# The last part of a fused convolution, attention and expert kernel: the way back to channels on VectorE, reciprocal roots on ScalarE, and a new order

## The chip, the cores and the metric

The kernel runs on one core of a Trainium2 chip. The metric is device time in microseconds for one execution of the whole program; lower is better. The core has five engines that run their own instruction streams in order and wait for each other through semaphores: TensorE (PE in the profile; its weight loads are PEld), VectorE (DVE), ScalarE (ACT), GpSimd (POOL) and SyncE (SP, which here only issues DMAs).

## The reference, cut to what matters

The input is 32 images of 128 channels by 64 x 64 pixels. Two layers follow each other.

```python
# layer 0: a convolution in a butterfly basis, after a group norm
x = x + _kop2d(_gn(x), weight, kd1, kd2, k11, k12, k21, k22)
# layer 1: tokens are pixels, 128 channels each
t = to_tokens(x)
t = t + attn(_ln_t(t), Wk, bk, Wv, bv)                 # one 128 x 128 softmax per image
t = t + experts(_ln_t(t), router_w, router_b, expert_w, expert_b)   # 8 experts, the best 2 per token
x = from_tokens(t, x)

def _ln_t(v, eps=1e-5):
    m = jnp.mean(v, axis=-1, keepdims=True)
    s = jnp.var(v, axis=-1, keepdims=True)
    return (v - m) / jnp.sqrt(s + eps)
```

All is fp32. `_ln_t` needs the reciprocal root of a variance for each token (pixel), twice per image.

## The kernel before, in words

The program has three parts. The first brings every image into the butterfly basis along both axes, the second mixes channels there, and the third, which the change is in, takes one image at a time through the inverse transform, the attention and the experts. Parts hand over through DRAM (`xf`, `pf`).

The third part has, for each image `b`, these steps; their names are the keys that the plan below uses.

- `r0` to `r7` load the mixed image, `x` loads the original one (the tile is called `y` there). `w0` to `w7` (PE, L877, tile `pu`) invert along one axis, and `wo` (ACT, L887) copies the result to `u`, in four copies for each `pu`. `h0` to `h3` (PE, L899, tile `py`) invert along the other axis; every `py` needs all of `u`. `ho` (DVE, L907) adds the result to the image. For the first two images smaller pieces do the same.
- `pt0` to `pt7` (PE, L1021) transpose the image to tokens, four tiles of 128 tokens at a time, `to` (ACT, L1026) copies them to `tk`, which holds 32 tiles of 128 tokens x 128 channels, and `sa` (DVE, L993) takes batch statistics. `va` (DVE, L1003 to L1008) makes variances of them, `pwa` (POOL, L1013) the power of -0.5, `na` (DVE, L1050, L1051) what the normalization needs.
- `xg` (ACT, L1061) normalizes, `pg` (PE, L1072) sums the 128 x 128 Gram matrix, and a short chain (`gs`, `pb`, `t1`, `pb2`, `sm`, `pr`, `sr`, `sn`, `pc`, `prx`) makes the softmax of the attention.
- `pp` (PE, L1145) applies it, three token tiles at a time, `at` (ACT, L1158, L1162) scales, `ad` (DVE, L1173, L993) adds to `tk` and takes statistics. `vb`, `pwb`, `nb` make the second reciprocal root as `va`, `pwa`, `na` made the first.
- `lg`, `l2`, `f1` to `f4`, `gt` (DVE, L1205 to L1248, with one exponential on ACT, `f5`) make the gates of the best two experts.
- `xn` (ACT, L1273) normalizes, `px` (PE, L1283) transposes, `xT` (ACT, L1289) copies. `pe` (PE, L1296) multiplies one token tile with four experts; there are 64 such halves per image. `m` (DVE, L1307) weighs each half by the gates into `tm`, and `s` (POOL, L1332 to L1335) sums over experts into `tk`, once for two token tiles.
- `st` (PE, L1342, tile `po`) transposes four finished token tiles back to channels, `so` (ACT, L1348) copies them out of PSUM, and a DMA on SP's queue stores 128 channels x 512 pixels.

PSUM is shared by three pools: `pe` (three banks), `cv` (one buffer of two banks, for `pu` and `py`) and `tl` (three banks, for `pt`, `px`, `pp`, `po` and the small ones).

Steps of neighbouring images run beside each other: while image `b` is at its convolution, `b - 1` is at its attention and `b - 2` at its experts. The order of instructions on each engine is written by a planner (class `Plan`). Each step has an engine, a cost in microseconds that the author gave it, a due time (`SLOT` times the image's number, an offset and the step's entry in the table `SHIFT`), the steps it comes after, and buffers that it takes and frees. The planner plays the steps through with those costs, lets each engine take the ready step with the earliest due time, and the program is then emitted in that order. On the chip only the order is left: an engine waits at its next instruction, whatever else is ready.

Of the kernel before, what the change touches and what calls it, by code (L numbers as in the profile page):

```python
# [12 lines left out]
ALU = mybir.AluOpType  # L13
# [77 lines left out]
def kernel(  # L91
# [674 lines left out]
    rp = ctx.enter_context(tc.tile_pool(name="rp", bufs=10))  # L766
    xp = ctx.enter_context(tc.tile_pool(name="xp", bufs=2))
# [31 lines left out]
    def prepare():  # L799
# [23 lines left out]
    plan = Plan({"cv": 1, "pe": 3, "tl": 3, "r": 10, "x": 2, "xg": NG, "xn": 2, "xT": 2, "tm": 2, "so": 2, "gate": 2})  # L823
# [3 lines left out]
        "ad": -0.15, "at": -0.25, "f": 0.71, "gs": -1.97, "gt": 0.71, "h": -0.24, "ho": -3.5, "kvp": 3.43,  # L827
        "kvq": -0.45, "l": 0.71, "lg": 3.61, "m": -0.32, "na": -1.87, "nb": -0.81, "pb": -1.97, "pc": -1.97,
        "pe": 0.16, "pg": -0.08, "pp": 0.19, "pr": -1.97, "prx": -1.97, "pt": -0.23, "pwa": -1.87, "pwb": 3.61,
        "px": 0.15, "r": -0.04, "s": 0.08, "sa": 1.29, "sm": -1.97, "sn": -1.97, "so": 2.13, "sr": -1.97,  # L830
        "st": 1.1, "t": -1.97, "to": 0.06, "va": -1.87, "vb": 3.61, "w": 0.28, "x": -0.68, "xT": -0.68,
        "xg": 0.21, "xn": 2.42,
# [12 lines left out]
    xs, rs, tile_of, first = {}, {}, {}, [prepare]  # L845
# [25 lines left out]
    def conv(b):  # L871
# [31 lines left out]

        def h_out(g):
            def run():
                acc = xs[b][:, :, 16 * g : 16 * g + 16]
                nc.vector.tensor_tensor(  # L907
                    acc, tile_of.pop(("cy", b, g)).rearrange("o (w h) -> o h w", h=n), acc, ALU.add
                )
            return run  # L910
# [33 lines left out]
        def h_out_piece(q):  # L944
            def run():
                acc = xs[b][:, :, 8 * q : 8 * q + 8]
                nc.vector.tensor_tensor(
                    acc, tile_of.pop(("cz", b, q)).rearrange("o (w h) -> o h w", h=n), acc, ALU.add
                )
            return run  # L950

        if b < 2:
# [10 lines left out]
            for g in range(4):  # L963
                for k in range(2):
                    at = b + 0.68 + 0.07 * g + 0.035 * k
                    h, ho = (f"h{g}", f"ho{g}") if k else (f"h{g}_0", f"ho{g}_0")
                    add(
                        b, h, "PE", 1.05, at, h_inverse_piece(2 * g + k),
                        [f"wo{e}_{oh}" for e in range(8) for oh in range(2)] + ([f"h{g}_0"] if k else []), ("pe",),
                    )  # L970
                    add(b, ho, "DVE", 0.7, at, h_out_piece(2 * g + k), [h, "x"] + ([f"ho{g}_0"] if k else []), (), ("pe",))
# [9 lines left out]
        for g in range(4):  # L981
            at = b + 0.68 + 0.07 * g
            add(b, f"h{g}", "PE", 2.05, at, h_inverse(g), [f"wo{e}_{oh}" for e in range(8) for oh in range(2)], ("cv",))
            add(b, f"ho{g}", "DVE", 1.2, at, h_out(g), [f"h{g}", "x"], (), ("cv",))

    def front(b):
# [24 lines left out]
        def power(which):  # L1011
            total, var, nmr, rstd = v[which]
            nc.gpsimd.tensor_tensor(rstd, var, mhalf, ALU.pow)  # L1013

        def turn(g):
            def run():
                ps = tile_of["pt", b, g] = tps.tile([P, 512], F32, tag="tl", name=f"pt{b}_{g}")
                x1 = xs[b].rearrange("c h w -> c (h w)")
# [21 lines left out]
        for g in range(8):  # L1040
            at = s1 + 0.016 * g
            add(b, f"pt{g}", "PE", 0.48, at, turn(g), [(b - 2, f"st{g}")] + [f"ho{k}" for k in range(4)], ("tl",))
# [3 lines left out]
        add(b, "pwa", "POOL", 5.5, s1 + 0.14, lambda: power(1), ["va"])  # L1046

        def nmr1():
            total, var, nmr, rstd = v[1]
            nc.vector.scalar_tensor_tensor(nmr, total, -0.5, rstd, ALU.mult, ALU.mult)  # L1050
            nc.vector.tensor_scalar_add(v["above"], nmr, 1.0)  # L1051

        add(b, "na", "DVE", 0.9, s1 + 0.14, nmr1, ["pwa"])
# [85 lines left out]
        def product(lo, m):  # L1139
            def run():  # L1140
                x1 = xs[b].rearrange("c h w -> c (h w)")
# [35 lines left out]
        for j, lo in enumerate(range(0, NT, 3)):  # L1177
            m = min(3, NT - lo)
            at = s1 + 0.45 + 0.016 * j
            add(b, f"pp{lo}", "PE", 0.26 * m, at, product(lo, m), ["prx", (b - 1, "lg")], ("tl",), ("x",) if lo == 30 else ())  # L1180
# [29 lines left out]
        def nmr2():  # L1210
            total, var, nmr, rstd = v[2]
# [41 lines left out]
        add(b, "pwb", "POOL", 5.5, at, lambda: power(2), ["vb"])  # L1253
        add(b, "lg", "DVE", 1.95, at, logits1, ["vb"])
        add(b, "nb", "DVE", 2.1, at + 0.1, nmr2, ["pwb", "lg"])
# [8 lines left out]
    def experts(b):  # L1264
# [73 lines left out]
        def back(g):  # L1338
            def run():
                ps = tile_of["po", b, g] = tps.tile([P, 512], F32, tag="tl", name=f"po{b}_{g}")  # L1340
                for k in range(4):
                    nc.tensor.transpose(ps[:, k * P : (k + 1) * P], t[:, 4 * g + k, :], ident)  # L1342
            return run

        def store(g):
            def run():
                so = wp.tile([P, 512], F32, tag="so", name=f"so{b}_{g}")
                nc.scalar.copy(so, tile_of.pop(("po", b, g)))  # L1348
                nc.sync.dma_start(ov[b][:, g * 512 : (g + 1) * 512], so)
# [3 lines left out]
        for g in range(8):  # L1353
# [25 lines left out]
            add(b, f"st{g}", "PE", 0.48, at + 0.25, back(g), [f"s{2 * g}", f"s{2 * g + 1}"], ("tl",))  # L1379
            add(b, f"so{g}", "ACT", 0.55, at + 0.25, store(g), [f"st{g}"], (), ("tl",))  # L1380
# [63 lines left out]
```

## Time and profile before

| what | value |
| --- | --- |
| median of 3 runs | 6059.13 us (6056.47 to 6059.99) |
| profiled execution, span | 6062.4 us |
| PE busy | 5891.6 us |
| DVE busy | 4221.2 us |
| POOL busy | 4191.0 us |
| ACT busy | 3756.5 us |

The span is the time from the first to the last instruction of one profiled execution. A busy time is the sum of the engine's own instructions; matmuls overlap, and their ends are modelled. In lists of groups the columns are: line, engine, operation, written tile `<-` read tiles, shape and count, then busy microseconds in sum and mean nanoseconds of one, then the engine's idle time just before them and who ended it. In lists by time the columns are start, duration, engine, line, operation, and in brackets the idle time before. A matmul in fp32 shows as two instructions, a transpose as one.

### The profile page before, as it was taken

The numbers are of one execution on the slowest core, as the hardware profiler recorded it, in microseconds if no ns is written. First come the engines' busy times: TensorE is split into PE (matmuls) and PEld (weight loads), VectorE is DVE, ScalarE is ACT, GpSimd is POOL, SyncE is SP. The second block draws the span as 40 slices with busy tenths as digits, with TensorE's granted clock in tenths as the row PEclk, the third lists the DMA queues.
The fourth block names the chain that finished last, engine by engine and source line by source line (L and its number), as shares of the span: only waits on it lengthen the run. The fifth ranks groups of instructions, "written<-read, shape, count | busy, mean of one in ns | idle before, by whom it ended". The sixth has DMA issues, their size and how long they took to land.

```text
span 6062.4 us, 219265 instructions
## 1 busy us (share of the span) xinstructions
PE 5891.6 (97%) x95372; PEld 4677.6 (77%) x95372; DVE 4221.2 (70%) x7696; ACT 3756.5 (62%) x7057; POOL 4191.0 (69%) x3765
## 2 busy tenths in 40 slices
PE   7999999999999999889999999999999999999998
PEld 7999999999999999776666666666666666666654
DVE  5565545555555555448878787787878878787878
ACT  7666664555555555366667667666766766676663
POOL 2110006666666666428898898989989898998988
PEclk9999999999999999999999999999999999999999
DMA  6767666666666666632313222231322223132100
GB/s 200 238 224 237 234 214 193 172 173 172 172 174 171 171 171 172 160 107 77 92 56 102 67 88 81 72 97 57 101 68 84 84 64 104 57 97 71 65 27 28
DMA packets 555044, 756.74 MB, mean 125 GB/s; under 512 B 58592, under 2 KB 319712, under 8 KB 549984
## 3 DMA queue, kind: packets, MB, share of 16 engines
q1 hardware_dynamic: 551856, 738.76, 41.0%
q8 instruction: 749, 12.27, 0.9%
q0 software_dynamic: 896, 2.62, 0.1%
q14 instruction: 215, 1.76, 0.1%
q10 hardware_dynamic: 1328, 1.32, 0.1%
HBM read 406.93 MB, written 335.54 MB: 122 GB/s over the span
## 4 chain that ended last, share of the span: by engine, by line
PE 88%; ACT 7%; issue 2%; DVE 1%; POOL 1%; DMA 1%; SPq 0%; ACTq 0%; POOLq 0%; DVEq 0%
PE pe L1296 28%; PE m L654 17%; PE g L632 9%; PE pf L418 7%; PE pu L877 6%; PE pp L1145 4%; PE py L899 4%; PE pg L1072 4%; PE pv L396 3%; PE px L1283 2%; ACT xn L1273 2%; ACT u L887 2%; PE pz L373 1%; PE pt L1021 1%; ACT z L383 1%
## 5 line engine op out<-in xcount | busy, mean ns | idle before, releaser
L1296 PE MATMUL pe<-ew_sb,xT 128*128 128x512 f32 x4096 | 1948.4, 597 | 18.6 <-DVE tm L1307 15.1
L1307 DVE TENSOR_TENSOR tm<-pe,oh 128x512 f32<-128x512 f32 x2028 | 1346.6, 684 | 478.9 <-PE pe L1296 456.6
L1332 POOL TENSOR_TENSOR tm<-tm 128x512 f32<-128x512 f32 x1014 | 1285.0, 1284 | 202.6 <-DVE tm L1307 199.3
L1296 PEld LDWEIGHTS pe<-ew_sb,xT 128*128 128x128 f32 x4096 | 701.6, 191 | 523.4 <-issue 400.1
L643 DVE COPY f<-g 128x1024 f32<-128x1024 f32 x508 | 622.3, 1225 | 644.4 <-PE g L632 644.2
L654 PE MATMUL m<-f,s 128*64 128x64 f32 x32768 | 1068.9, 224 | 1.1 <-ACT f L643 0.8
L654 PEld LDWEIGHTS m<-f,s 128*64 128x64 f32 x32768 | 999.0, 138 | 62.4 <-issue 1.5
L600 POOL COPY s<-l 128x512 f32<-128x512 f32 x512 | 547.2, 1105 | 526.4 <-issue 509.7
L643 ACT COPY f<-g 128x1024 f32<-128x1024 f32 x508 | 514.7, 1013 | 556.4 <-PE g L632 530.1
L1335 POOL TENSOR_TENSOR tk<-tk,tm 128x256 f32<-128x256 f32 x1014 | 753.9, 743 | 79.5
L1333 POOL TENSOR_TENSOR tm<-tm 128x512 f32<-128x512 f32 x507 | 650.3, 1283 | 39.8
L887 ACT COPY u<-pu 64x512 f32<-64x512 f32 x960 | 556.3, 579 | 135.1 <-PE pu L877 121.6
L632 PE MATMUL g<-c,wst 9*128 9x128 f32 x16256 | 599.6, 283 | 1.7 <-issue 1.5
L632 PEld LDWEIGHTS g<-c,wst 9*128 9x128 f32 x16256 | 503.0, 186 | 36.2 <-issue 1.5
L349 POOL TENSOR_TENSOR grstd<-gms,mhalf 128x1 f32<-128x1 f32 x32 | 17.8, 555 | 737.8 <-DVE gms L345 737.8
L1158 ACT ACTIVATE pp<-pp,m 128x128 f32<-128x128 f32 x1024 | 440.9, 431 | 124.2 <-PE pp L1145 99.2
L602 POOL TENSOR_SCALAR s<-l 128x512 f32<-128x512 f32 x256 | 511.3, 1997 | 0.0
L877 PEld LDWEIGHTS pu<-qw,r 128*128 128x128 f32 x3840 | 455.1, 193 | 62.8 <-ACT u L887 49.0
L877 PE MATMUL pu<-qw,r 128*128 128x128 f32 x3840 | 475.8, 277 | 25.1 <-ACT u L887 25.1
L1289 ACT COPY xT<-px 128x512 f32<-128x512 f32 x256 | 150.2, 587 | 563.2 <-PE px L1283 560.1
L418 PE MATMUL pf<-ph,v 128*128 128x128 f32 x4096 | 491.2, 278 | 6.2 <-issue 1.4
L418 PEld LDWEIGHTS pf<-ph,v 128*128 128x128 f32 x4096 | 467.0, 192 | 16.0 <-ACT z L383 7.1
(169 smaller groups left out, 8569.6 us busy)
## 6 DMA issues: line engine op xcount, KB each, us to landing
xf<-f SPq DMA_DIRECT2D x512, 256.0 KB, 3.3
pf<-o SPq DMA_DIRECT2D x1024, 128.0 KB, 3.3
l<-xf SPq DMA_DIRECT2D x1012, 128.0 KB, 3.2
r<-pf SPq DMA_DIRECT2D x504, 256.0 KB, 4.7
x<-in_x_dram SPq DMA_DIRECT2D x256, 256.0 KB, 4.5
y<-in_x_dram SPq DMA_DIRECT2D x32, 2048.0 KB, 9.3
out_dram<-so SPq DMA_DIRECT2D x256, 256.0 KB, 2.2
tw<-in_tw_dram SPq DMA_DIRECT2D x6, 384.0 KB, 7.5
```

Of the source, the lines that this page charges most:

```text
L418: nc.tensor.matmul(pl[:, j * P : (j + 1) * P], vs[b][:, 8 * g + j, :], ph.rearrange("h r m -> h (r m)"), start=True, stop=True,)
L600: nc.gpsimd.tensor_copy(dst, src)
L632: nc.tensor.matmul(pg[g // 2][:, g % 2, m * P : (m + 1) * P], wst[rows, 16 * half + 4 * t + m, :], c[rows].rearrange("r h k -> r (h k)"), ...
L643: copy(f.rearrange("i m (g o) -> i m g o", g=2), tile_of["g", w, half, t][k].rearrange("i g (o m) -> i m g o", o=4))
L654: nc.tensor.matmul(ps[hh * n : (hh + 1) * n, q, :], s[:, h].rearrange("i k b -> i (k b)")[:, B * r : B * r + n], f[:, h, r, :], start=(r = ...
L877: nc.tensor.matmul(ps[:, k, :], rs[b, e][:, k * P : (k + 1) * P], qw.rearrange("w r m -> w (r m)"), start=True, stop=True,)
L887: nc.scalar.copy(u[r * n : (r + 1) * n, :, oh * n + 8 * e : oh * n + 8 * e + 8], ps[oh * n : (oh + 1) * n, :, r * n : (r + 1) * n].rearran ...
L1296: nc.tensor.matmul(ps, tile_of["xT", b, i // 4][:, i % 4, :], ew_sb[:, es, :].rearrange("d e c -> d (e c)"), start=True, stop=True,)
L1307: nc.vector.tensor_tensor(tile_of["tm", b, i // 2][:, i % 2, es, :], tile_of.pop(("pe", b, i, half)).rearrange("p (e c) -> p e c", c=P), t ...
L1332: nc.gpsimd.tensor_tensor(tm[:, k, 0:4, :], tm[:, k, 0:4, :], tm[:, k, 4:8, :], ALU.add)
L1333: nc.gpsimd.tensor_tensor(tm[:, :, 0:2, :], tm[:, :, 0:2, :], tm[:, :, 2:4, :], ALU.add)
L1335: nc.gpsimd.tensor_tensor(t[:, lo : lo + 2, :], t[:, lo : lo + 2, :], tm[:, :, m, :], ALU.add)
```

## The change

It has three pieces. The way back to channels leaves PE and ACT: `so` becomes a block transpose on DVE, which swaps rows and columns inside blocks of 32 x 32, from `tk` straight to the tile that is stored, and a new step `os` on SP stores it with four DMAs. For this the pixels stand in another order within a token tile (4 rows of the image x 32 columns), so that `ho` no longer adds in place but writes a new tile, and the pools change: `r` 10 to 7 buffers, `x` 2 to 1, and a new pool `y` of 2. The power of -0.5 leaves POOL: ACT makes the exponential of -0.5 times the logarithm, and DVE refines it by one Newton step of three operations, ahead of `na` and `nb`. And the table `SHIFT` of due places is new.

```diff
-    rp = ctx.enter_context(tc.tile_pool(name="rp", bufs=10))
-    xp = ctx.enter_context(tc.tile_pool(name="xp", bufs=2))
+    rp = ctx.enter_context(tc.tile_pool(name="rp", bufs=7))
+    xp = ctx.enter_context(tc.tile_pool(name="xp", bufs=1))
+    yp = ctx.enter_context(tc.tile_pool(name="yp", bufs=2))
...
-    plan = Plan({"cv": 1, "pe": 3, "tl": 3, "r": 10, "x": 2, "xg": NG, "xn": 2, "xT": 2, "tm": 2, "so": 2, "gate": 2})
+    plan = Plan({"cv": 1, "pe": 3, "tl": 3, "r": 7, "x": 1, "y": 2, "xg": NG, "xn": 2, "xT": 2, "tm": 2, "so": 2, "gate": 2})
...
     SHIFT = {
-        "ad": -0.15, "at": -0.25, "f": 0.71, "gs": -1.97, "gt": 0.71, "h": -0.24, "ho": -3.5, "kvp": 3.43,
...
+        "ad": 1.200, "at": 4.424, "f": -1.562, "gs": 5.457, "gt": 1.265, "h": 3.849, "ho": 0.837, "l": 3.501,
+        "lg": 4.916, "m": -6.559, "na": -1.525, "nb": 2.094, "os": -8.513, "pb": -14.726, "pc": -5.745,
+        "pe": 0.195, "pg": -3.978, "pp": 0.047, "pr": 3.687, "prx": 0.077, "pt": 0.017, "pwa": -4.729,
+        "pwb": 2.491, "px": 0.184, "r": 2.416, "s": 18.080, "sa": 3.764, "sm": -3.600, "sn": -3.745,
+        "so": 2.421, "sr": 3.337, "t": -3.008, "to": -4.337, "va": -9.740, "vb": 0.270, "w": 2.015, "wo": 4.100,
+        "x": 9.338, "xT": 4.479, "xg": -7.285, "xn": 5.672,
     }
...
+        def added(ps, lo, m):
+            if lo == 0:
+                ys[b] = yp.tile([P, 16, 2, 4, 32], F32, tag="y", name=f"x1_{b}")
+            wh, j = divmod(lo, 32)
+            nc.vector.tensor_tensor(
+                ys[b][:, :, wh, :, j : j + m].rearrange("o l a w -> o a l w"),
+                ps.rearrange("o (w a l) -> o a l w", a=4, w=m),
+                xs[b][:, :, lo : lo + m].rearrange("o (a l) w -> o a l w", a=4), ALU.add,
+            )
...
         def power(which):
             total, var, nmr, rstd = v[which]
-            nc.gpsimd.tensor_tensor(rstd, var, mhalf, ALU.pow)
+            nc.scalar.activation(rstd, var, AF.Ln)
+            nc.scalar.activation(rstd, rstd, AF.Exp, scale=-0.5)
+
+        def newton(which):
+
+            total, var, nmr, rstd = v[which]
+            nc.vector.scalar_tensor_tensor(var, var, -0.5, rstd, ALU.mult, ALU.mult)
+            nc.vector.tensor_tensor(var, var, rstd, ALU.mult)
+            nc.vector.scalar_tensor_tensor(rstd, var, 1.5, rstd, ALU.add, ALU.mult)
...
-        add(b, "pwa", "POOL", 5.5, s1 + 0.14, lambda: power(1), ["va"])
+        add(b, "pwa", "ACT", 0.55, s1 + 0.14, lambda: power(1), ["va"])
...
-        add(b, "pwb", "POOL", 5.5, at, lambda: power(2), ["vb"])
+        add(b, "pwb", "ACT", 0.55, at, lambda: power(2), ["vb"])
...
-        def back(g):
-            def run():
-                ps = tile_of["po", b, g] = tps.tile([P, 512], F32, tag="tl", name=f"po{b}_{g}")
-                for k in range(4):
-                    nc.tensor.transpose(ps[:, k * P : (k + 1) * P], t[:, 4 * g + k, :], ident)
+        def flip(g):
+            def run():
+                so = tile_of["so", b, g] = wp.tile([P, 4, 4, 32], F32, tag="so", name=f"so{b}_{g}")
+                nc.vector.transpose(
+                    out=so.rearrange("p k t w -> p t k w"),
+                    in_=t[:, 4 * g : 4 * g + 4, :].rearrange("p t (k c) -> p t k c", c=32),
+                )
             return run
 
         def store(g):
             def run():
-                so = wp.tile([P, 512], F32, tag="so", name=f"so{b}_{g}")
-                nc.scalar.copy(so, tile_of.pop(("po", b, g)))
-                nc.sync.dma_start(ov[b][:, g * 512 : (g + 1) * 512], so)
+                so = tile_of.pop(("so", b, g)).rearrange("p k t w -> p k (t w)")
+                for a in range(4):
+                    nc.sync.dma_start(
+                        ov[b][:, a * 1024 + g * P : a * 1024 + (g + 1) * P].rearrange("(k c) m -> c k m", c=32),
+                        so[32 * a : 32 * a + 32],
+                    )
             return run
...
-            add(b, f"st{g}", "PE", 0.48, at + 0.25, back(g), [f"s{2 * g}", f"s{2 * g + 1}"], ("tl",))
-            add(b, f"so{g}", "ACT", 0.55, at + 0.25, store(g), [f"st{g}"], (), ("tl",))
+            add(b, f"so{g}", "DVE", 0.62, at + 0.25, flip(g), [f"s{2 * g}", f"s{2 * g + 1}"], ("so",))
+            add(b, f"os{g}", "SP", 0.2, at + 0.25, store(g), [f"so{g}"], (), ("so",), 4.0)
```

## The prediction, made before the changed kernel ran

> **What bounds the kernel now.** I read the page's span and busy shares first, then the busy times by stretch, the chain that ended last, the groups of the last part with shapes kept apart, and the instructions of one image in order of time on TensorE and ScalarE.
>
> ```profile
> span 6062.4 us, 219265 instructions
> ...
> PE 5891.6 (97%) x95372; PEld 4677.6 (77%) x95372; DVE 4221.2 (70%) x7696; ACT 3756.5 (62%) x7057; POOL 4191.0 (69%) x3765
> ```
>
> The shares mix three parts. The change is in the last one, from about 2550 us on. Of the steady stretch there, by engine (500 us, so 4.7 images):
>
> ```profile
> core 0: us, PE busy (x) PEld busy (x) DVE busy (x) ACT busy (x) POOL busy (x), PEclk, DMA share, GB/s
> 4500.00:5000.00 500.00, 493.83 (x3543) 337.19 (x3542) 398.06 (x884) 340.75 (x787) 446.94 (x388) 1.00 0.24 74
> ```
>
> PE is busy 98.8%, POOL 89%, DVE 80%, ACT 68%, DMA 24%. The chain that ended last repeats with one image; the same piece comes back after 106.37 us:
>
> ```profile
> 3944.92 5.15 PE pe L1296 x12
> ...
> 4051.29 5.15 PE pe L1296 x12
> ```
>
> So the last part is 106.37 us per image, and PE is what the images share. How much of it is work? In the order of time on PE each matmul group starts before the modelled end of the one before it, so I take start to start:
>
> ```profile
> 4048.03 0.60 PE L1283 MATMUL px<-ident,xn 128*128 128x128 f32 x4
> 4048.47 0.60 PE L1342 MATMUL po<-ident,tk 128*128 128x128 f32 x4
> 4048.90 1.95 PE L877 MATMUL pu<-qw,r 128*128 128x128 f32 x16
> 4050.69 0.60 PE L1021 MATMUL pt<-ident,y 128*128 128x128 f32 x4
> ```
>
> A group of four transposes takes 0.435, a `pu` 1.79. In the same way one `pe` half takes 0.86, `py` 2.02, `pg` 0.885, `pp` 0.735 (the last, of two, 0.49), `pb` and `pc` together 0.7. Per image: 64 x 0.86 + 8 x 1.79 + 4 x 2.02 + 8 x 0.885 + 7.84 + 0.7 + 24 x 0.435 (`px`, `pt`, `po`) = 103.4 us. PE thus waits 3.0 us of 106.4.
>
> **The change part by part.**
>
> ```profile
> L1013 POOL TENSOR_TENSOR m<-m,mhalf 128x32 f32<-128x32 f32 x64 | 348.3, 5442 | 156.6 <-DVE m L1008 156.6
> L1342 PE MATMUL po<-ident,tk 128*128 128x128 f32 x1024 | 155.0, 274 | 8.0 <-POOL tk L1335 7.4
> L1348 ACT COPY so<-po 128x512 f32<-128x512 f32 x256 | 144.4, 591 | 129.6 <-PE po L1342 126.2 <-DMA out_dram<-so 1.5 <-ACT xn L1273 1.1
> L1220 DVE TENSOR_TENSOR eq<-eq,rank 128x256 f32<-128x256 f32 x64 | 84.8, 1325 | 2.2
> L1212 DVE SCALAR_TENSOR_TENSOR m<-m 128x32 f32<-128x32 f32 x32 | 38.1, 1191 | 0.2 <-POOL m L1013 0.2
> L1207 DVE TENSOR_TENSOR eq<-m,rws 128x256 f32<-128x256 f32 x32 | 13.9, 435 | 0.0
> L1204 DVE SCALAR_TENSOR_TENSOR m<-m,m 128x32 f32<-128x32 f32 x32 | 6.3, 198 | 0.0
> ```
>
> *The way back.* Gone per image are 8 `po` groups on PE, 8 x 0.435 = 3.5 us on the path, leaving 99.9 us of PE work. ACT loses 8 x 0.59 = 4.7. DVE gets 8 block transposes of 128x512, an operation that this trace lacks. From below: DVE's own copy of 128x1024 (from PSUM) takes 1225 ns (L643), so 0.6 us. From above: ops that read SBUF beside a busy POOL show what a collision costs (L1220 takes 1325 ns where L1207, the same shape, takes 435), so 0.6 + 0.9 = 1.5. I take 0.6, since the transpose has one input like the copy and the batch statistics (`bs`, 280 ns for 128x128 out of SBUF), which show no such delay. That adds 5 us to DVE's 84.7. The Trainium skill ("VectorE: DVE Perf Modes", The three transpose paths) gives 311 ns for a 128x128 bf16 tile by 32x32 blocks; four of these make 1.24 us, an estimate by that page, which would add another 5 us to DVE, more than the 3.5 us that PE saves, if DVE sets the pace.
>
> *The add of the convolution* (`ho`) now reads `x` and writes `y` in another order of pixels; it reads PSUM at a stride as before and stays one element per element, so I leave it at L907's 1225 ns.
>
> *Stores.* One DMA of 2 KB rows becomes four of 512 B pieces: SP issues one in 0.34 to 0.5 us, so 1.4 to 2.0 instead of 0.34, and `out` now lands 2.2 us after the last. With two `so` buffers and a flip per two POOL sums (2 x 5.4 us) it is hidden by that spacing; without it a flip would wait some 4 us. In the built order SP puts the load of the next `y` and one `r` ahead of the fourth store; both wait for work (`ho3`, `pu0`) that PE and DVE do before that flip. I price it at nothing, and the smaller pools (`r` 7, `x` 1) too: `r7` of an image can load from `pu0` on, tens of us ahead of `pu7`.
>
> *Roots.* POOL loses 2 x 5.44 = 10.9 us per image and falls from 95 to 84, so the sums `s` stop being held back. DVE gets 6 small Newton operations, 0.2 us each by L1204 and up to 1.2 by L1212: 1.2 to 7, I take 2.2 since some meet POOL. ACT gets a logarithm and an exponential of 128x32, 0.23 each (L1239's duration). And in the built order of the changed kernel a table load stands before each of them: 4 per image, 128 more in all, where before has a single one:
>
> ```profile
> 10.30 1.28 ACT L360 ACT_TABLE_LOAD   x1 [10.30 <-DVE gbs L319]
> 20.01 4.64 ACT L360 ACTIVATE x<-x,gnmr,grstd 128x1024 f32<-128x1024 f32 x4 [8.43 <-POOL gnmr L353]
> ```
>
> The row is 1.28 us; what follows it there is a wait for POOL, so it shows no cost behind the load, only that this is under 8.4 us. ACT's shortest steps are 0.19 (L1107's read of the accumulator), so I take 1.28 and keep 1.5 as the upper end; from below, a load that runs while ACT waits anyway is free. So `pwa` and `pwb` take ACT 2 x 1.28 + 2 x 0.23 = 3.0 us each, while the plan that made the order counts 0.55. ACT has the room in sum (73 - 4.7 + 6 = 74 of 106), but it runs in order. Who stands behind?
>
> At `pwb` ACT's next are `to2`, `xT6`, `to3`; PE has 8 `pe` halves and one `pu` (8.7 us) before it needs `to2`. Hidden.
>
> At `pwa` it isn't. The built order for images 5 to 18, from the end of `pt7` as zero: PE has 4 `pe`, `px`, `pu7`, 4 `pe` (0.43 + 8 x 0.86 + 1.79 = 9.1 us), then `py0`, which needs all of `u`. ACT has `to7`, `xT2` (waits for that `px`, done about 4.1), `xn4` 1.6, `pwa` 3.0, and only then the four copies of `pu7` (2.4 us by `u` at 580 ns): 4.1 + 0.5 + 1.6 + 3.0 + 2.4 = 11.6. PE waits 2.5 us. With 0.55 in place of 3.0 it would not wait at all. Images 2 to 4 and 19 to 30 have `py0` earlier and `xn4` after `pwa`: PE has `pe` x3, `px`, `py0`, `pe` x4 = 8.5 us before `pg0`, which needs `to7` 0.8, then the statistics and moments on DVE (to about 4.6), two loads and two functions (part of the first load earlier, done about 6.9), Newton 2.2 and `xg0` 1.7 = 10.8. PE waits 2.3. In before the same place shows ACT idle and PE not:
>
> ```profile
> 4091.30 1.65 ACT L1273 ACTIVATE xn<-tk,m 128x128 f32<-128x128 f32 x4
> 4095.58 12.43 ACT L1061 ACTIVATE xg<-tk,m 128x128 f32<-128x128 f32 x32 [2.64 <-DVE m L1051]
> ```
>
> A rule of the Trainium skill speaks against this part ("ScalarE: Activation LUTs", What ACT_TABLE_LOAD costs): each switch is 1283 ns, which the trace has, and then a drain of about 1380, which no row here shows; by it `pwa` would be 5.8 us, PE's wait 5.1, and the whole some 80 us worse.
>
> *The refitted order.* PE's other waits were 3.0. In the new order `py1` to `py3` stand between `pp` groups with only three `pe` in reach: 18.7 us of PE work against DVE's 9 x 1.18 (add and statistics) + 3 x 1.15 (`ho`) + 3 x 0.6 + one flip = 16.5, begun 2.5 late. And the top-2 blocks on DVE (5.4, 4.0 and 3.6 us) no longer have `po` beside them, only three `pe` banks and the `pu`. Each costs about 1, so I take 5.2 in place of 3.0; as before and 7 are the bounds.
>
> Sum: 99.9 + 5.2 + 2.4 = 107.5 per image, against 106.37: +1.1 to +1.4, over 30 images +35 to +42. The tail of two images has two powers of 5.45 on the chain; each becomes some 4, so -3. Against the profiled execution: 6062.4 + 38 = 6100; the span stands 3.3 above the median of the runs, 6059.1, so that makes 6097; rounded 6100 us, with 6070 to 6145 as this case's own range.
>
> **Rivals.** *PE keeps its gain* (the other side). The ACT queue is ahead of PE by more than I count, so `py0` and `pg0` find their inputs ready, and PE's waits stay at 3.0: 102.9 per image, 5955 at best; with 1 to 2 us of waits left, 5985 to 6015. For it: ACT idles 32%, and POOL's relief of 10.9 us takes the waits of `tm` away. Against: `xT2` ties ACT to a `px` that stands just ahead. It decides where added waits stay under 3.5 us per image.
>
> *DVE becomes the bound.* Flips and Newton steps meet POOL as L1220 and L1212 do: five of eight flips lie where DVE is late, 5 x 0.9 = 4.4, and Newton 4 more, half of it on the path: +2 to +5 per image over my sum, 6160 to 6240. For it: DVE goes from 80% to 86% on my price already. Against: one-input rows show no such delay.
>
> *The change does less than it says:* the root's steps may land on hidden work altogether and the gain of `po` be eaten by the new order alone; this is the no-change case, 6047 to 6071.
>
> **How the numbers follow.** Forecast 0.42, DVE as bound 0.25, PE keeps its gain 0.27, no change 0.06. A measurement of this kernel can tell about 0.2%, 12 us. Slower is 0.42 + 0.25 = 0.67, same 0.06, faster 0.27. The range leaves out the best of the gain and the worst of the DVE case: 5985 to 6205.
>
> **What would show it.** Right: 129 table loads of 1.28 us; PE waiting 2 to 3 us on ACT `u` before `py0` (later images: on `xg` before `pg`); no wait at `pwb`; a period near 107.5; POOL near 80%. The transposes near 0.6 us. Wrong: PE without such waits and a period under 105, or transposes at 1.2 us and PE waiting for DVE `tm` all over the image.

## The result, and the profile after

The changed kernel takes 6257.4 us (median of 4 runs, 6254.9 to 6267.2) against 6058.3 before: a ratio of 1.033 (95% interval 1.0316 to 1.0344), 199 us slower. The forecast was 6100 us with a range to 6205; it had the direction and missed the size. The profiled execution took 6267.2 us with a span of 6265.5.

The page's span and busy shares:

```profile
span 6265.5 us, 218587 instructions
...
PE 5920.2 (94%) x94348; PEld 4617.2 (74%) x94348; DVE 4602.7 (73%) x8144; ACT 3798.7 (61%) x7057; POOL 3855.4 (62%) x3701
```

Against the page of before POOL has lost 335.6 us of work and DVE gained 381.5. The steady stretch by engine, 500 us of it:

```profile
core 0: us, PE busy (x) PEld busy (x) DVE busy (x) ACT busy (x) POOL busy (x), PEclk, DMA share, GB/s
4500.00:5000.00 500.00, 468.18 (x3116) 308.69 (x3115) 433.23 (x887) 332.28 (x743) 376.28 (x356) 0.98 0.25 75
```

PE is down from 98.8% to 93.6%, DVE up from 80% to 87%, POOL down from 89% to 75%. From one `gs` copy on DVE to the next, the mean period of an image is 113.7 us, where before had 106.6 in the same count: 30 intervals x 7.0 = 211, which is the whole of the loss (the span grew by 203). The period is 116.0 for most of images 4 to 17 and 110.4 to 111.6 after. PE's groups start at the same distances as before where nothing holds them up (0.86 for a `pe` half, 1.78 for a `pu`), so its work is 99.9 us per image, as forecast, and PE now loses 13.8 us per image instead of 3. Most of that is waiting; in images 4 to 17 the granted clock is lower too (0.96 in most of them, 0.98 to 1.00 in the later ones; the last section comes back to it). Waiting for what? PE's and its weight loads' waits of the last part, first in the trace after, then in that of before, both from 2700 to 5900 us (columns: us in total, times, longest):

```profile
PEld pe L1318 <- DVE tm L1329: 395.3, 587, 2.4
...
PE pe L1318 <- DVE tm L1329: 191.5, 182, 2.0
```

```profile
PEld pe L1296 <- DVE tm L1307: 33.6, 98, 5.3
...
PE pe L1296 <- DVE tm L1307: 8.4, 4, 5.0
```

PE waits for DVE to empty the `pe` banks. The waits that the forecast named, for ACT's `u` before `py0` and for `xg`, are not there. One image (5335.5 to 5445.9) by stretches of 5 us, four of its rows:

```profile
5375.50:5380.50 5.00, 5.00 (x25) 3.12 (x24) 5.00 (x17) 2.23 (x5) 4.84 (x5) 1.00 0.11 27
5380.50:5385.50 5.00, 2.98 (x19) 2.30 (x19) 4.83 (x9) 2.52 (x5) 3.16 (x4) 1.00 0.42 124
...
5405.50:5410.50 5.00, 3.62 (x21) 2.53 (x20) 4.90 (x7) 1.52 (x3) 4.84 (x5) 1.00 0.13 34
...
5440.50:5445.50 5.00, 5.00 (x36) 4.04 (x36) 2.38 (x4) 3.81 (x10) 4.84 (x5) 1.00 0.16 39
```

The third number after the length is DVE. From 5365.5 to 5435.5, the 70 us from the end of the attention's adds through the gates to the Gram matrix of the next image, its rows sum to 67.5: 96%, while in the last row, beside `pg`, it is busy 48%. A mean of 87% hides a stretch in which DVE is the bound, and PE's waits of 1.4 to 2.0 us stand in it. In before DVE's idle time (18.5 us in the image that I followed, in gaps of 0.2 us and more) is spread over 21 gaps all around the image.

What DVE does there is also slower than before. Groups of the last part, after:

```profile
L1363 DVE STREAM_TRANSPOSE so<-tk 128x512 f32<-128x512 f32 x256 | 178.8, 699 | 0.0
...
L1248 DVE TENSOR_TENSOR lg<-lg,rb_sb 128x256 f32<-128x256 f32 x32 | 43.1, 1346 | 1.1
...
L1269 DVE TENSOR_TENSOR oh<-oh,oh 128x256 f32<-128x256 f32 x32 | 42.5, 1329 | 1.1
...
L1228 DVE TENSOR_TENSOR eq<-m,rws 128x256 f32<-128x256 f32 x32 | 37.3, 1164 | 0.0
...
L1227 DVE TENSOR_TENSOR lg<-lg,lq 128x256 f32<-128x256 f32 x32 | 35.4, 1108 | 1.1
```

The transposes take 0.70. The others existed before, and took 843, 827, 435 and 455 ns there. Summed over the last part and divided by 32 images, DVE's work is 103.1 us per image against 90.7 (the recorded durations of neighbouring operations overlap a little, so the busy time by stretches is less: 96.8 us in the image above, 85.5 in one of before). Of the 12.4 more, 5.6 are transposes, 2.4 the six Newton operations (0.85, 0.92 and 0.67 per image for the three lines), and 4.4 the net growth of operations that the change does not touch. The four first logit operations (L1226 to L1229) grew by 2.6 us per image and the moments (L1015 to L1020, twice per image) by 3.4, while others became shorter (L1220 of before, for one, lost 1.05). Two lines of the moments, after and before:

```profile
L1016 DVE TENSOR_TENSOR m<-bs 128x32 f32<-128x32 f32 x64 | 45.3, 707 | 0.0
...
L1018 DVE TENSOR_TENSOR m<-m 128x32 f32<-128x32 f32 x64 | 43.3, 677 | 0.0
```

```profile
L1004 DVE TENSOR_TENSOR m<-bs 128x32 f32<-128x32 f32 x64 | 15.3, 238 | 0.0
...
L1006 DVE TENSOR_TENSOR m<-m 128x32 f32<-128x32 f32 x64 | 12.8, 200 | 0.0
```

The order of time shows how an operation grows. DVE, then POOL, at the same moment:

```profile
5379.50 1.54 DVE L1226 TENSOR_TENSOR lg<-lq,m 128x256 f32<-128x256 f32 x1
5381.07 1.37 DVE L1227 TENSOR_TENSOR lg<-lg,lq 128x256 f32<-128x256 f32 x1
5382.37 0.94 DVE L1228 TENSOR_TENSOR eq<-m,rws 128x256 f32<-128x256 f32 x1
```

```profile
5378.26 2.49 POOL L1354 TENSOR_TENSOR tm<-tm 128x512 f32<-128x512 f32 x2
5380.83 1.33 POOL L1355 TENSOR_TENSOR tm<-tm 128x512 f32<-128x512 f32 x1
5382.24 0.79 POOL L1357 TENSOR_TENSOR tk<-tk,tm 128x256 f32<-128x256 f32 x1
```

POOL's instructions end at 5380.75, 5382.16 and 5383.03; DVE's end at 5381.04, 5382.44 and 5383.31, each 0.28 to 0.29 us later. One small DVE operation gets through per POOL instruction. The same operations in before, and what POOL did then:

```profile
4049.90 0.42 DVE L1205 TENSOR_TENSOR lg<-lq,m 128x256 f32<-128x256 f32 x1
4050.35 0.42 DVE L1206 TENSOR_TENSOR lg<-lg,lq 128x256 f32<-128x256 f32 x1
```

```profile
4048.17 5.44 POOL L1013 TENSOR_TENSOR m<-m,mhalf 128x32 f32<-128x32 f32 x1 [0.59 <-DVE m L1008]
```

They took their shortest time, 0.42, beside the power. The power cost POOL 10.9 us per image and sheltered DVE's logits meanwhile. Ahead of each power POOL stood idle until the moments were done (156.6 us in 64 waits, the row of L1013 in the prediction), so in before few sums ran beside the moments either.

### The profile page after: what moved, and what is told of

Same layout as the page of the kernel before. It is cut to its first block, busy times and chain, and to the rows that moved or that the text cites. A ratio compares the mean times of both kernels' runs of the same rounds, so it can differ in the third digit from the quotient of the medians.

```text
span 6265.5 us, 218587 instructions
## 1 busy us (share of the span) xinstructions
PE 5920.2 (94%) x94348; PEld 4617.2 (74%) x94348; DVE 4602.7 (73%) x8144; ACT 3798.7 (61%) x7057; POOL 3855.4 (62%) x3701
## 4 chain that ended last, share of the span: by engine, by line
PE 67%; DVE 21%; ACT 7%; issue 3%; DMA 1%; POOL 0%; SPq 0%; ACTq 0%; DVEq 0%; POOLq 0%
PE m L654 16%; PE pe L1318 16%; PE g L632 9%; DVE tm L1329 7%; PE pf L418 6%; PE pg L1093 4%; PE pp L1166 4%; PE py L900 3%; PE pv L396 3%; DVE bs L1005 3%; PE pu L878 3%; ACT pp L1179 1%; PE pz L373 1%; ACT z L383 1%; ACT u L888 1%
## 5 line engine op out<-in xcount | busy, mean ns | idle before, releaser
L1318 PE MATMUL pe<-ew_sb,xT 128*128 128x512 f32 x4096 | 2003.7, 618 | 241.3 <-DVE tm L1329 229.7
L1329 DVE TENSOR_TENSOR tm<-pe,oh 128x512 f32<-128x512 f32 x2028 | 1324.7, 681 | 333.9 <-PE pe L1318 312.6
L1318 PEld LDWEIGHTS pe<-ew_sb,xT 128*128 128x128 f32 x4096 | 729.3, 196 | 946.9 <-DVE tm L1329 460.1
L878 PEld LDWEIGHTS pu<-qw,r 128*128 128x128 f32 x3840 | 480.1, 201 | 90.8 <-ACT u L888 53.0
L878 PE MATMUL pu<-qw,r 128*128 128x128 f32 x3840 | 502.3, 287 | 15.3 <-ACT u L888 15.3
L1005 DVE BATCH_NORM_STATS2 bs<-tk 128x6 f32<-128x128 f32 x2048 | 449.8, 279 | 20.3 <-ACT tk L1046 8.0
```

Source lines behind the costliest of these rows:

```text
L878: nc.tensor.matmul(ps[:, k, :], rs[b, e][:, k * P : (k + 1) * P], qw.rearrange("w r m -> w (r m)"), start=True, stop=True,)
L1005: nc.vector.bn_stats(bs[:, i].rearrange("p a s -> p (a s)"), t[:, i, :])
L1318: nc.tensor.matmul(ps, tile_of["xT", b, i // 4][:, i % 4, :], ew_sb[:, es, :].rearrange("d e c -> d (e c)"), start=True, stop=True,)
L1329: nc.vector.tensor_tensor(tile_of["tm", b, i // 2][:, i % 2, es, :], tile_of.pop(("pe", b, i, half)).rearrange("p (e c) -> p e c", c=P), t ...
```

## The experiments

Theory A: VectorE sets the pace in that long stretch; what the change put there, and the collisions with GpSimd's sums, set the loss. The rivals were ScalarE's table loads (the forecast's own mechanism), the new order, and, later, TensorE or GpSimd. The time of the changed kernel is 6257.4 throughout; "before" is the kernel before on the same chip; runs with an interval were timed four times, the others once. The changed kernel's own runs span 12 us, and before took 6058 to 6067 in these series, so a difference of some 10 us tells nothing.

| run | us | before | ratio (95%) | DVE us per image |
| --- | --- | --- | --- | --- |
| e1 power back | 6429.4 | 6065.0 | | 102.6 |
| e2 no Newton | 6180.2 | 6065.0 | | 101.1 |
| e3 no table switch | 6246.0 | 6065.0 | | 103.3 |
| e4 no flip | 6248.8 | 6065.0 | | 96.2 |
| e5 less POOL | 6069.7 | 6062.2 | | 92.3 |
| e6 old places | 6348.0 | 6062.2 | | 95.1 |
| e7 flips alone, old places | 6431.5 | 6062.2 | | 94.8 |
| e8 roots alone, old places | 6166.8 | 6062.2 | | 92.1 |
| e9 no flip, free stores | 6223.4 | 6065.9 | 1.026 (1.025-1.028) | 97.9 |
| e10 power planned | 6291.7 | 6065.9 | 1.037 (1.036-1.039) | 98.1 |
| e11 bare | 6166.4 | 6065.9 | 1.017 (1.015-1.018) | 96.2 |
| e12 costs told | 6403.9 | 6065.9 | 1.057 (1.055-1.058) | 97.3 |
| e13 short sums | 6179.2 | 6067.3 | 1.019 (1.017-1.020) | 99.8 |
| e14 three logit ops out | 6161.5 | 6067.3 | 1.016 (1.014-1.017) | 101.5 |
| e15 attention add out | 6212.4 | 6067.3 | 1.024 (1.022-1.026) | 97.5 |
| e16 short sums, no Newton | 6110.8 | 6067.3 | 1.007 (1.005-1.008) | 96.7 |
| e17 four gates on ACT | 6146.6 | 6062.4 | 1.014 (1.012-1.015) | 94.5 |
| e18 eight gates on ACT | 6164.7 | 6062.4 | 1.017 (1.015-1.018) | 92.1 |

**The roots: e1, e2, e3, e8.** e1 puts the power back on POOL in the order that the change made:

```diff
-            nc.scalar.activation(rstd, var, AF.Ln)
-            nc.scalar.activation(rstd, rstd, AF.Exp, scale=-0.5)
+            nc.gpsimd.tensor_tensor(rstd, var, mhalf, ALU.pow)
```

> The changed kernel with its order held as it is, but the power of -0.5 on POOL again and no Newton step. Theory A (VectorE sets the pace in the half of each image between the first transpose to tokens and the first convolution add, and each microsecond of VectorE work there goes onto the period): VectorE loses 2.4 us of Newton per image, and its small two-input operations, which took 3.9 us per image longer than before, fall back in part, since POOL's power does not collide with them as its sums do; 4 to 6 us per image, so 6065 to 6135 us, with L1226 to L1229 back near 0.42 us. Theory B (the forecast's: the four table loads hold ScalarE's copies and PE waits for those): 2.4 us per image, some 6185 us, and the small operations of VectorE stay as slow as in the changed kernel.

It took 6429. The power now stands behind sums in POOL's queue, and DVE, then ACT wait for it:

```profile
ACT xg L1079 <- DVE m L1069: 221.4, 28, 8.6
...
DVE m L1068 <- POOL m L1025: 112.9, 28, 4.4
```

Of the four logit operations only the first is back at 0.41 us; the others take 1.07 to 1.20, against the expectation, and DVE's sum hardly fell. The run tells what an order is worth to one engine's steps, and nothing of the roots. e2 leaves the three lines of `newton` out:

> The changed kernel in its order, with the three Newton operations left out (the root stays less exact); the table loads stay. Theory A: 2.4 us of VectorE per image in the saturated half, 29 images, some 75 us less, 6180 us. Theory B: the Newton step lies behind the loads and hardly counts, 6240 us or more.

It took 77 us less for 2.4 us of DVE work per image. That is 2.5 us per image, a full price on the mean (more on that below, with e14). e3 replaces `AF.Ln` by `AF.Identity`, so that no table is switched:

> The changed kernel in its order, with the logarithm replaced by a plain copy function (so the root is wrong), which leaves no table load but the first. Theory A: the loads lie on ScalarE beside VectorE's work; only the later images, where the chain shows load and exponential between the moments and the Newton step, gain about 1.5 us each, 13 of them: 20 us, 6235 us. Theory B: 2.3 to 2.6 us per image, 6185 us.

It took 11 us less: 128 loads of 1.28, 164 us of ACT, are worth 11 at most, which is within the spread of the runs. The loads are not the cause. e8 is the kernel before, its order table kept, with only the roots changed (the planner, told the new steps, writes its order anew):

> The kernel before with the roots alone changed (logarithm, exponential and Newton step), due places as before. Theory A: VectorE gets 2.4 us of Newton and 2 to 4 us of collisions that the power on POOL had kept away, about 91 of 106 us: 6080 to 6200 us. Theory B: 2 x 3.0 us of loads and functions on ScalarE, PE waits 2.5 us per image: 6135 us, and VectorE's small operations as fast as before.

It took 105 us more than before. Its four first logit operations, at 0.42 to 0.46 in before, show the lost shelter without the flips (groups of e8):

```profile
L1214 DVE TENSOR_TENSOR lg<-lq,m 128x256 f32<-128x256 f32 x32 | 42.5, 1327 | 0.0
...
L1215 DVE TENSOR_TENSOR lg<-lg,lq 128x256 f32<-128x256 f32 x32 | 42.0, 1313 | 1.1
...
L1216 DVE TENSOR_TENSOR eq<-m,rws 128x256 f32<-128x256 f32 x32 | 30.2, 945 | 0.0
...
L1217 DVE TENSOR_TENSOR lg<-lg,eq 128x256 f32<-128x256 f32 x32 | 25.7, 804 | 1.1
```

That is 4.4 us per image where before had 1.74, for POOL work that was taken away. DVE's sum grew by only 1.4 us per image, though, Newton included, since other operations became shorter; the 105 us are not a matter of DVE's sum. PE's and its weight loads' waits for `tm` (2700 to 5900 us) rose from 42 to 254 us, and DVE's waits for the roots from ACT are 9 us in all, so here too it is a late DVE and not the loads.

**The flips: e4, e9.** e4 leaves the transpose out and stores from `tk`:

> The changed kernel in its order, with the block transposes left out: the stores read the token tiles as they are, so the output is not turned back. Theory A: five of eight transposes lie in VectorE's saturated half, 5 x 0.63 = 3.1 us per image, up to 5.0 for all eight: 95 to 150 us less, 6107 to 6160 us. Theory B: VectorE has room, 6240 us or more.

It took 9 us less, which is inconclusive, since a new wait came with it, of the next image's copy for the store:

```profile
ACT tk L1046 <- DMA out_dram<-tk: 161.4, 48, 5.5
```

e9 mends that: the stores read a tile that nothing writes.

```diff
-                so = tile_of.pop(("so", b, g)).rearrange("p k t w -> p k (t w)")
+                so = still
```

> The changed kernel without the block transposes on VectorE; the four stores of a group read one fixed tile of SBUF that nothing writes, so that, unlike in e4_no_flip, no later step waits for a store (the values stored are left out). Theory A (VectorE sets the pace in half of each image): the transposes' 5.6 us per image leave the path there, of which some 3.5 lie in that half, and TensorE's waits and their loss of clock shrink with it: 6110 to 6170 us, period 108 to 110 in later images. Rival B (the transposes lie in gaps of VectorE): within 20 us of 6257.

It took 34 us less for 5.6 us of DVE work per image. Theory A was wrong in size: per microsecond of DVE work the flips cost a fifth of what Newton costs. In images 18 to 29 the period hardly moved (110.7 for 111.0). A DVE operation that comes earlier may only wait longer for the same POOL instruction; that would explain it, and was not shown.

**The collisions: e5, e13.** e5 leaves two of POOL's five adds per sum out:

```diff
-                for k in range(2):
-                    nc.gpsimd.tensor_tensor(tm[:, k, 0:4, :], tm[:, k, 0:4, :], tm[:, k, 4:8, :], ALU.add)
```

> The changed kernel in its order, with two of POOL's five operations per sum left out (the sums over the upper four experts are wrong), so that POOL is busy for 2.8 instead of 5.4 us per sum. Theory A with collisions (VectorE's small operations with both operands in SBUF wait for POOL's sums, 3.9 us per image more than before, nearly all in the half where VectorE sets the pace): most of these 3.9 us and some of the Newton's go, 100 to 150 us less, 6110 to 6160 us, L1226 to L1229 well under their 1.0 to 1.16 us. Rival (POOL has idle time, so its length does not matter): within 20 us of 6257.

It took 188 us less, as much as nearly the whole loss, though flips, Newton and table loads are all in it. DVE's waits for POOL are small in the changed kernel (13.7 us in all at `tm`), so it is the collisions that went: DVE fell by 10.8 us per image, as L1269 from 1329 to 616 ns. But less POOL work could help in other ways too, so e13 keeps all of it and shortens its instructions:

```diff
-                    nc.gpsimd.tensor_tensor(tm[:, k, 0:4, :], tm[:, k, 0:4, :], tm[:, k, 4:8, :], ALU.add)
+                    for e in (0, 2):
+                        nc.gpsimd.tensor_tensor(tm[:, k, e : e + 2, :], tm[:, k, e : e + 2, :], tm[:, k, e + 4 : e + 6, :], ALU.add)
```

(and the third add, one per token tile in the same way).

> The whole change, with GpSimd's adds of 128x512 done as two of 128x256 each (8 instructions of some 0.74 us per sum in place of 5, GpSimd's work 5.95 in place of 5.3 us per sum, 9.8 us per image more). Everything else is held. Theory A (a small VectorE operation whose inputs are all in SBUF waits until GpSimd's running instruction ends, and these waits set the period): the waits get shorter with the instruction, VectorE falls by 3 to 5 us per image and the time by 80 to 150 us: 6105 to 6180. Rival B (the two share the bandwidth, whatever the instruction's length, or GpSimd's throughput sets the pace): 6257 or slower.

It took 78 us less with 7.8 us more POOL work per image (92.1 for 84.3). The groups of e13 that were 1108, 1346 and 1329, then POOL's halved add:

```profile
L1248 DVE TENSOR_TENSOR lg<-lg,rb_sb 128x256 f32<-128x256 f32 x32 | 26.2, 820 | 1.1
...
L1269 DVE TENSOR_TENSOR oh<-oh,oh 128x256 f32<-128x256 f32 x32 | 26.2, 819 | 1.1
...
L1227 DVE TENSOR_TENSOR lg<-lg,lq 128x256 f32<-128x256 f32 x32 | 26.2, 819 | 1.1
```

```profile
L1355 POOL TENSOR_TENSOR tm<-tm 128x256 f32<-128x256 f32 x2028 | 1458.8, 749 | 623.9 <-DVE tm L1329 607.2 <-DVE tops L1266 12.1
```

All at 0.82, POOL's instruction of 0.75 and the 0.07 to the next one. Shared bandwidth would not give three operations one and the same time that follows the other engine's instruction length. This is shown: they wait for the end of the running instruction. Not shown is how much of these gains is loss that the change brought: small operations of the kernel before collide too (843 and 827 ns above), and no run halves or leaves out the sums there.

**Where DVE's time counts: e14, e15.** Twins. e14 leaves three of the four first logit operations out (L1227 to L1229, inside the 70 us), e15 the add of the attention's product (L1194, ahead of them):

```diff
-            nc.vector.tensor_add(lg, lg, lq[:, :, 1, :])
-            nc.vector.tensor_tensor(eq, by_expert(nmr), by_token(rws), ALU.mult)
-            nc.vector.tensor_add(lg, lg, eq)
```

> The changed kernel with three of the four operations that make the first logits left out (1.11, 1.17 and 1.06 us of VectorE per image in the trace). They stand in the stretch from the last add of the attention to the first add of the convolution, where VectorE has no gap. Theory A (VectorE sets the pace in that stretch): 3.3 us per image come off the period, some 100 us: 6130 to 6175. Rival B (VectorE only looks full there, GpSimd's or TensorE's pace sets it): within 35 us of 6257.

```diff
-                nc.vector.tensor_tensor(t[:, lo : lo + m, :], ps[:, :, 0:P], t[:, lo : lo + m, :], ALU.add)
```

> The twin of e14: the changed kernel with the adds of the attention's product left out on VectorE (11 per image, 5.9 us; the statistics still read the tokens), which stand in the other stretch, where VectorE has gaps and TensorE sets the pace. Theory A: little comes off though it is nearly twice the work of e14: 6210 to 6257. Rival B (VectorE's total work sets the time, wherever it stands): 6257 less 5.9 x 31 = 183, 6075.

They took 96 us less for 3.3 us per image inside, and 45 less for 5.9 outside: 0.93 against 0.25 of the period for each microsecond (divided by 31 images). So the place counts. It is not DVE's share that tells the two places apart, though. In the image above eight of the eleven adds of the attention stand in the 15 us from 5345.5 on, and DVE has no more room there (97%); but PE is busy throughout and shows no wait:

```profile
5345.50:5350.50 5.00, 5.00 (x76) 3.55 (x74) 4.86 (x13) 4.29 (x13) 4.76 (x6) 1.00 0.22 55
5350.50:5355.50 5.00, 5.00 (x92) 4.72 (x89) 4.93 (x13) 3.07 (x9) 3.39 (x4) 1.00 0.00 0
5355.50:5360.50 5.00, 5.00 (x88) 4.56 (x87) 4.79 (x14) 4.11 (x13) 0.00 (x0) 1.00 0.15 33
```

Nor is every operation in the 70 us worth the same: five of the image's eight flips stand there, and e9 took all eight out for 34 us. The prices also mix two kinds of image. What each run took off the period, by the `gs` copies:

| run | work left out, us per image | images 4 to 17 | images 18 to 29 |
| --- | --- | --- | --- |
| e2 Newton | 2.4 | 4.6 | 1.8 |
| e14 three logit ops | 3.3 | 5.2 | 2.3 |
| e15 attention add | 5.9 | 2.8 | 1.2 |
| e9 flips | 5.6 | 2.2 | 0.35 |

From 3100 to 4500 us the granted clock is 0.96 in the changed kernel, 0.99 in e2 and e14 and 0.98 in e15 and e9; from 4800 to 5800 it is 0.99 to 1.00 in all five. In the later images a microsecond is worth 0.75, 0.70, 0.20 and 0.06 in these four runs: the order of the prices stays, and what the means have above it comes from the images with the low clock.

**The order: e6, e7, e10, e11, e12.** e6 is the whole change with the old table `SHIFT`; e7 the flips with the old table and the power on POOL; e10 the flips with the new table and the power on POOL, with its cost told to the planner.

> The whole change, but with the due places of the kernel before. Theory C (the new due places are to blame: they crowd transposes, roots and routing on VectorE into one half of the image): 6150 us or less. Theory A (VectorE's work is the same, 12 us more per image than before, whatever the order): 6220 to 6300 us.

> Only the way back by block transposes, with the power on POOL and the due places of the kernel before. PE loses 3.5 us per image, VectorE gains 5.6 and stays under 91 of 103. If the roots are what costs: 5960 to 6060 us. If the transposes cost as much by themselves: over 6100 us.

> The changed kernel with its new due places, the power back on GpSimd (5.5 us) and no Newton step, and here the plan is told both costs, so that the order is made for them (in e1_pow_back the order was held). Theory A: VectorE's load falls by Newton's 2.4 us and the small operations beside the power are fast again, but GpSimd stands at 95 of 106 us and holds the sums back: 6150 to 6300. Rival B (only the held order made e1 slow, and the transposes alone pay): under 6059.

They took 6348, 6432 and 6292 us. The old places are worse with this work than the new ones; whether a third order would do better is open. DVE has only 95 to 98 us per image in all three, so DVE's sum does not set these times, and in e10 the logits are back at 0.45 to 0.50 us, most of them started beside the power. What is late in e7 is spread over ACT's and POOL's queues (ACT waits 394 us for PE at `u`, 306 at `tk`; POOL 146 us for the moments), and I did not follow it to one cause. e12 tells the planner the durations of the trace (3.0 for each root on ACT, 2.6 and 3.8 for the steps with Newton, 4.8 for the first logits):

> The whole change, with the plan told the durations of the trace: 3.0 us for each root on ScalarE, 2.9 for the moments, 2.6 and 3.8 for the steps with Newton, 4.8 for the first logits, 0.7 for a transpose. Nothing else is changed; the order follows. Theory A (the work on VectorE sets the pace, whatever the order): 6200 to 6300. Rival B (the plan's wrong costs made a bad order): under 6150.

It took 6404 us, with periods from 89 to 143 us. Both theories missed: truer costs gave a worse order. That the due times had been fitted to the old costs may be why; it was not tested. e11 takes flips, Newton steps and table switches out together and keeps the order:

> As e9_no_flip_free, and also without the Newton step and with Identity in place of the logarithm, so that no table loads are left but one (the root's values are left out). What remains is the changed kernel's order, its four stores and TensorE's saved transposes, without the VectorE and ScalarE work that they were paid with. Theory A (added VectorE work and its collisions set the loss): VectorE some 95 us per image, period 104 to 106.5, 6000 to 6080. Rival B (the new order itself costs it): over 6120.

It took 6166 us, not under 6080. Theory A fell here in its first form: the added work makes 91 us of the 199, and 100 stay with TensorE's saving still in. DVE keeps 96.2 us per image, 5.5 more than before, all of it existing operations. It is this run that pointed to collisions as the larger half, and e13 came from it; how the 100 divide between collisions and the new order itself was not measured.

**Towards a better version: e16, e17, e18.** e16 joins e13 and e2.

> e13_short_sums and e2_no_newton together: GpSimd's long adds in halves and the root by logarithm and exponential alone. Theory A: both take work off VectorE in the same stretch, so the gains add up: 6257 - 77 - 80 to 150, 6030 to 6100, near the kernel before. Rival B (TensorE's own waits on ScalarE take over once VectorE is relieved): 6120 to 6180.

It took 147 us less, where the two alone gave 78 + 77 = 155. That is nearly additive, but 11 us above the expected range and still 0.7% slower than before. e17 and e18 move some gate multiplications of the stretch from DVE to ACT:

```diff
+                        nc.scalar.activation(
+                            tile_of["tm", b, i // 2][:, i % 2, 4 + e, :], ps[:, e * P : (e + 1) * P], AF.Identity,
+                            scale=tile_of["gate", b][:, i, 4 + e : 5 + e],
+                        )
```

> e16_short_sums_no_newton, and four of the 64 gate multiplications of an image (tokens' blocks 2, 21, 25 and 29, second half), all in the stretch where VectorE has no gap, are done by ScalarE: four operations of 128x128 out of PSUM, about 1.6 us per half, beside 0.64 us on VectorE that go. Theory A: VectorE's stretch falls by 2.6 us per image, ScalarE has idle time there: 6111 less 50 to 80, 6030 to 6060. Rival B (ScalarE's queue is late for the copies that TensorE needs, and PE waits on it instead): 6111 to 6180.

> As e17_four_gates_on_act with eight such multiplications (blocks 1, 3, 20, 22, 24, 26, 28 and 30), 5.1 us less on VectorE and some 13 us more on ScalarE per image. Theory A: VectorE's stretch comes under TensorE's work there, so the gain stops near 6111 - 110 to 150: 5960 to 6000. Rival B: ScalarE's queue costs PE more than VectorE gives back: 6111 to 6250.

DVE's work fell as meant (96.7 to 94.5 and 92.1), and the time rose by 36 and 54 us. Four operations of 0.37 us on ACT hold a `pe` bank longer than one of 0.68 on DVE. PE's and its weight loads' waits for `tm` stay (378 us in e16, 396 in e17, from 2700 to 5900), and DVE waits more for POOL to free `tm` (waits of e16, then of e17):

```profile
DVE tm L1327 <- POOL tk L1357: 104.5, 79, 2.4
```

```profile
DVE tm L1335 <- POOL tk L1365: 151.2, 114, 2.5
```

So it seems that relief of DVE pays only where it does not lengthen the step from bank to sum; no run lengthens that step alone. ACT's `u` was not it in e17 (PE's wait there stays near 20 us). No version here beats the kernel before.

## Why the prediction was wrong

*PE's own work*: right. 99.9 us per image, `po` gone (the terms of the sum for before add up to 103.5, not 103.4, which changes nothing).

*The direction was luck.* It hung on the 2.4 us for the table loads: without them the sum is 99.9 + 5.2 = 105.1, under the 106.37 of before, a forecast of faster. That wait does not exist (e3).

*The term that failed is "PE's other waits", 5.2 us with bounds 3 and 7.* Together with the 2.4 us forecast for the loads it made 7.6; the trace has 13.8. The 6.2 us between them, over 30 images, make 186, a little more than the 165 by which the forecast missed the span; what the first and last images gave back was not followed. Of the 186, images 4 to 17 make 67 by being longer than the later ones (115.8 for 111.0), which the forecast had no term for. I asked whether DVE's sum would exceed the image (86% on my price) and looked for a late DVE in two short places, 1 us for each block. What showed in its place is PE waiting for DVE to empty the `pe` banks in a stretch of 70 us (191.5 us against 8.4 in before, and 395.3 against 33.6 for its weight loads, from 2700 to 5900). The mean of an engine over an image says nothing of a stretch; a table by stretches of before would have shown how near DVE was there (in an image of before, in the 35 us from 3949.9 on, DVE is busy 32.8).

*DVE's sum* was forecast to grow by 5 + 2.2 = 7.2 us per image (from the 84.7 busy in 500 us of before to 91.9) and grew by 12.4 (from 90.7 to 103.1, summed over operations). Flips 5.6 and Newton 2.4 were sized right; operations that the diff does not touch, +4.4 net, were missing. I had the rows for it: L1220 at 1325 and L1207 at 435 for one shape, and I used them to bound the new operations only. I noted that POOL loses 10.9 us and counted it as relief, without asking what ran beside it. e8 shows that loss without the flips: 2.6 us per image on four operations.

*A rule that speaks to this.* DVE and POOL in lockstep, as above, with 0.42 us free and 0.82 or 1.1 to 1.35 beside adds of 0.75 or 1.28. The Trainium skill ("SBUF — State Buffer", Who interferes with whom) has it: a VectorE instruction with two SBUF inputs contends with a GpSimd instruction that reads SBUF, and the ports that the two share are locked by one of them at a time. The trace agrees, with one exception: the power, two inputs out of SBUF and 5.44 us long, blocked none of the four.

*Loads*: 128 in the last part, 1283 ns each, as forecast; the wait at `pwa` is not there. Removing the switching is worth 11 us at most (e3), where the forecast had 2.4 x 30 = 72. The drain behind a load that the Trainium skill gives ("ScalarE: Activation LUTs", What ACT_TABLE_LOAD costs) is not there either (ACT's instructions in order):

```profile
5206.12 1.28 ACT L1026 ACT_TABLE_LOAD   x1
5207.42 0.23 ACT L1026 ACTIVATE m<-m 128x32 f32<-128x32 f32 x1
```

The next function starts 0.02 us after the load. *`pwb`*: no wait, right. *Transposes*: 0.70, near the 0.6 taken and far from the 1.24 worked out from the skill's page; they do not collide. *Stores at nothing*: right, the flips show 0.0 idle before them. *POOL*: 84 us of work per image, as forecast, and 75% where near 80 was said, since the period is longer; its relief shows as waiting for DVE (676 us at `tm`).

*The rival "DVE becomes the bound"* had the mechanism, with a price (6160 to 6240) that stops 17 us short: it let flips and Newton collide, and the flips don't, while the old operations do. What the forecast held against it, that one-input rows show no delay, was true of copies and statistics but not of all rows of before. Both of these have one input and the same shape:

```profile
L1244 DVE TENSOR_SCALAR tops<-tops 128x32 f32<-128x32 f32 x32 | 37.3, 1166 | 9.0 <-ACT tops L1239 9.0
...
L1051 DVE TENSOR_SCALAR m<-m 128x32 f32<-128x32 f32 x32 | 5.8, 181 | 1.1
```

The rival deserved more than 0.25 against 0.42.

## What to carry to other kernels

Read an engine's share by stretches of one image, not as a mean, and beside it what the pacing engine waits for: VectorE was 96 and 97% busy in two stretches of the same image, and a microsecond of it cost 0.93 where TensorE waited for it and 0.25 where TensorE was busy throughout. Even the first price is not one for all: the transposes, five of eight in that stretch, cost 0.2. Where GpSimd work is taken away, list what ran beside it; the slow power was the one GpSimd instruction here that let VectorE's small operations pass. Where GpSimd must run beside small VectorE operations with both inputs in SBUF, try shorter GpSimd instructions, even at more GpSimd time: here 7.8 us more of it per image brought 78 us in all.

## What the runs showed of the hardware that was not expected

A short wait of TensorE may cost twice. In an image with a period of 116, after waits of 1.4 to 1.9 us, the granted clock is low for 4 us or more (0.57 to 0.72 at the lowest, in stretches of 4 us). Two stretches of 4 us, and TensorE's instruction in them:

```profile
3140.00:3144.00 4.00, 2.15 (x17) 1.82 (x16) 3.97 (x7) 3.93 (x8) 3.43 (x4) 0.98 0.11 32
3144.00:3148.00 4.00, 4.00 (x7) 1.60 (x6) 3.13 (x7) 3.43 (x6) 2.95 (x3) 0.60 0.33 101
```

```profile
3143.56 5.40 PE L1318 MATMUL pe<-ew_sb,xT 128*128 128x512 f32 x8 [1.85 <-DVE tm L1329]
```

The clock column is the one after POOL: 0.60. Eight `pe` took 5.40 us, and 3.60 elsewhere in that image. In the later image shown above, waits as long left the clock at 1.00, and its period is 110.4. The two kinds of image differ by 5.6 us with DVE's busy time nearly equal (99 and 97 us); that the clock makes this difference fits, but no run changed it alone.
